# Reordering side tasks and partial products in a fused graph-attention kernel

## The chip, the cores and the metric

The kernel runs on one core of a Trainium2 chip. The metric is the device time of one execution in microseconds (us). Where two kernels are compared by a ratio, it is the mean time of one kernel's runs over the mean of the other's runs of the same rounds on the same chip, with a 95% interval. It is therefore not quite the quotient of the medians that stand beside it.

Engines: PE is TensorE (matrix products), DVE is VectorE, ACT is ScalarE, POOL is GpSimd, and SP is SyncE, whose queue (SPq) issues nearly all loads. An engine here starts its instructions in the order of its queue; what that costs is measured below (a write on VectorE that could have begun at 476.0 us began at 479.31, behind a norm that waited).

## The reference, cut to what matters

```python
# x: [128 graphs, 64 nodes, 512], float32; adj: [64, 64]
h = relu(layernorm(x))                           # input norm
def gat(h, W, a):                                # once with 4 heads, then once with 1
    Wh = h @ W
    e = leaky_relu(Wh @ a_left + (Wh @ a_right).T)
    return softmax(where(adj > 0, e, -1e9)) @ Wh
h   = elu(gat(h, W_heads, a_heads))              # 4 heads x 512 -> 2048 wide
out = elu(gat(h, W_out, a_out))                  # back to 512
y   = relu(out @ w1 + b1) @ w2 + b2 + out        # feed-forward
return x + layernorm(y) * gamma + beta           # gamma is 1 and beta 0 in these inputs
```

## The kernel before

The rows of x are cut into 64 tiles of 128 rows, four tiles to a group, 16 groups. A group passes through attention weights, a first projection (unit a, four heads), a second projection (unit b, 28 parts) and a feed-forward (units c and d). Products of 512 by 512 are made of seven smaller products instead of eight (numbered 1 to 7) with sums and differences of quarters around them; one small product is 8 matmuls. `unit` issues the seven in a given order and says what becomes of each:

```python
def after(p):                     # p: the product that has just been issued
    if p in (1, 5, 6):
        if p == 6:                # add product 1 to bank 6 (VectorE); then the copy "t"
            nc.vector.tensor_tensor(gb[6], gb[6], sb["s1"], ALU.add)
        nc.scalar.copy(sb[nm], gb[p])             # product 7 adds into bank 6 after this
        post(nm, sb[nm])
    elif p == 2: post("c11", gb[1])
    elif p == 7: post("c22", gb[6], sb["s5"], gb[1])   # an add on VectorE
    elif p == 3: post("c12", gb[5], sb["t"], gb[5])
    else:        post("c21", gb[6])                # product 4, in bank 6 behind c22's add
```

In unit a, product 4 of a head is issued only behind the second product of the next head. `run(steps, side)` spreads a list of side tasks evenly between the steps of a unit, and `mix` interleaves lists evenly. During the second projection of group g the side tasks are the feed-forward of group g-1 with its output norms, the attention sums of group g+1, and the input norms, scores, softmaxes and transposes of group g+2:

```python
# stage_a(g): side tasks of a later group; p and r are its two pairs of tiles
return [norms(p), norms(r), transposes(p), transposes(r), wait, project_f(g), wait, wait,
        (scores1(g), attn_weights(p)), None, attn_weights(r), wait, wait,
        transpose_weights(p), wait, wait, transpose_weights(r)]      # (shortened)
...
run(project2(g), mix(attn, tr) + mix(ff[:at] + early + ff[at:], stage_a(g + 2)) + fin)
```

`attn_weights` is a softmax on VectorE and ends with writing the weights `s1A`, which have one buffer. `transpose_weights` is a set of 8 transposes of `s1A` on TensorE (tile `s1pt`). `fin` are the four output norms, 7 instructions each:

```python
def finish(j):
    xr = load(t, "xr")                                     # the residual, on SyncE's queue
    nc.gpsimd.tensor_tensor(xr, xr, bs, ALU.add)           # the sum, GpSimd
    mean, rstd = norm_stats(y, "n2", t)                    # VectorE; the root (n2rs) on GpSimd
    nc.vector.scalar_tensor_tensor(y, y, mean, gs, ALU.subtract, ALU.mult)
    nc.vector.scalar_tensor_tensor(y, y, rstd, xr, ALU.mult, ALU.add)
    nc.sync.dma_start(out=of[ts(t, P), :], in_=y)
```

Of the kernel before, what the change touches and what calls it, by code (L numbers as in the profile page):

```python
# [22 lines left out]
def gat_preln_kernel(  # L23
# [38 lines left out]
    G = 4  # L62
# [178 lines left out]

    late = []

    def flush_late():
        while late:
            late.pop(0)()
# [148 lines left out]
    def scores1(g):  # L395

        L, R = LR.pop(g)
        pe = [aux([P, 2, H * N], f"s1pe{g}_{a}") for a in range(2)]
        for q in range(2):
            for a in range(2):  # L400
                for b in range(NB):
                    rows, cols = slice(64 * a, 64 * a + 64), slice(b * N, (b + 1) * N)
                    nc.tensor.matmul(
                        pe[a][cols, q, :].rearrange("p (h m) -> p h m", h=H), L[rows, q, cols],
                        R[rows, :, cols], start=(q == 0), stop=True, skip_group_check=True,
                    )
        for a in range(2):
            E1[2 * g + a] = pe[a].rearrange("p t (h m) -> p (t h) m", m=N)
# [67 lines left out]

    def stage_a(g):

        if g >= NG:
            return []  # L480
        p, r = 2 * g, 2 * g + 1

        def norms(p):
            norm1(2 * p)
            norm1(2 * p + 1)
            if p >= 2:
                prefetch(2 * p + 2)
                prefetch(2 * p + 3)

        def transposes(p):  # L490
            transpose_h(2 * p)
            transpose_h(2 * p + 1)

        wait = [lambda: None]
        return [
            lambda: norms(p), lambda: norms(r), lambda: transposes(p), lambda: transposes(r),
        ] + wait + [lambda: project_f(g)] + wait * 2 + [
            lambda: (scores1(g), attn_weights(p)), lambda: None, lambda: attn_weights(r),
        ] + wait * 2 + [lambda: transpose_weights(p)] + wait * 2 + [lambda: transpose_weights(r)]


    ZB = {}
# [54 lines left out]
    def project1(g, h):  # L557


        z = ZB[g]  # L560
        first = (g, h) == (0, 0)
        if h == 0:
            for b in ("11", "12", "S1", "22"):
                tag = "hS" if b == "S1" else "h" + b
                H1[b] = big.tile([P, H, 2, T], FP, tag=tag, name=f"h{b}_{g}")
        sums = {6: 0, 7: 1, 3: 2}
        blk = {1: "11", 2: "12", 4: "22", 5: "S1"}

        def post(what, a, b=None, to=None):
            if what[0] != "c":  # L570
                return
            nm = {"c11": "11", "c12": "12", "c21": "S1", "c22": "22"}[what]
            dst = H1[nm][:, h]
            if b is not None:
                nc.vector.tensor_tensor(to, a, b, ALU.add)  # L575
                a = to
            elu(flat(dst), flat(a), f"{what}_{g}_{h}")
            if what == "c21":
                nc.gpsimd.tensor_tensor(dst, dst, H1["22"][:, h], ALU.add)  # L579

        s = unit(
            f"a{g}_{h}", product_t(h, lambda p: ZSUM[h][sums[p]] if p in sums else z[blk[p]][:, h]),
            post, (1, 2, 6, 5, 7, 3, 4) if first else (1, 6, 5, 2, 7, 3, 4),
        )

        def next_sums():
            if h + 1 < H:
                z_sums(g, h + 1)

        return [  # L590
            s[0], lambda: (s[1](), flush_late()), lambda: (s[2](), next_sums()), s[3], s[4],
            lambda: (s[5](), late.append(s[6])),
        ]
# [90 lines left out]
    def feed_forward(g):  # L684

        o = OUT[g]
        OT, RT = [], []

        def transpose_out(j):
            if j % 2 == 0:  # L690
                OT.append(big.tile([P, KC, T], FP, tag=f"ot{j // 2}", name=f"ot{j // 2}_{g}"))
            pt = aux([P, KC, P], f"pto{g}_{j}")
            for k in range(KC):
                nc.tensor.transpose(pt[:, k, :], o[:, j, ts(k, P)], ident)  # L694
            nc.scalar.copy(OT[j // 2][:, :, ts(j % 2, P)], pt)
            nc.gpsimd.tensor_tensor(o[:, j], o[:, j], b2s, ALU.add)
            if j == G - 1:
                bl[1] = blocks(OT, f"o{g}")

        def blocks(tt, name):  # L700
            s2, s3, s4 = new_sums(name)
            a11, a12 = tt[0][:, 0:2], tt[0][:, 2:4]
            s1, a22 = tt[1][:, 0:2], tt[1][:, 2:4]
            nc.vector.tensor_tensor(s1, s1, a22, ALU.add)
            sums(nc.vector, s1, a11, a12, a22, s2, s3, s4)
            return {1: a11, 2: a12, 3: s4, 4: a22, 5: s1, 6: s2, 7: s3}

        bl = {}

        def post1(what, a, b=None, to=None):  # L710
            if what[0] != "c":
                return
            if not RT:
                RT.extend(big.tile([P, KC, T], FP, tag=f"rt{i}", name=f"rt{i}_{g}") for i in range(2))
            r, c = quadrant(what)
            dst = RT[r][:, 2 * c:2 * c + 2]
            if b is not None:
                nc.vector.tensor_tensor(dst, a, b, ALU.add)
                a = dst
            for k in range(2):  # L720
                nc.scalar.activation(
                    dst[:, k], a[:, k], AF.Relu, bias=b1s[:, 2 * c + k:2 * c + k + 1]
                )
            if what == "c21":
                bl[2] = blocks(RT, f"r{g}")

        def post2(what, a, b=None, to=None):

            if what == "s1":
                return  # L730
            r, c = {"t": (0, 1), "s5": (1, 1)}.get(what) or quadrant(what)
            dst = o[:, 2 * r:2 * r + 2, c * Q:(c + 1) * Q]
            eng = nc.vector if what[0] == "c" else nc.gpsimd
            eng.tensor_tensor(dst, a, dst, ALU.add)  # L734

        def finish(j):
            t = G * g + j
            xr = load(t, "xr")
            nc.gpsimd.tensor_tensor(xr, xr, bs, ALU.add)
            y = o[:, j]  # L740
            mean, rstd = norm_stats(y, "n2", t)
            nc.vector.scalar_tensor_tensor(y, y, mean, gs, ALU.subtract, ALU.mult)
            nc.vector.scalar_tensor_tensor(y, y, rstd, xr, ALU.mult, ALU.add)  # L743
            nc.sync.dma_start(out=of[ts(t, P), :], in_=y)

        f1 = unit(f"c{g}", product_t(M1, lambda p: bl[1][p]), post1, (1, 2, 6, 5, 7, 3, 4))
        f2 = unit(f"d{g}", product_n([M2], lambda p, i: bl[2][p]), post2, (1, 6, 5, 2, 3, 7, 4))
        return (
            [lambda j=j: transpose_out(j) for j in range(G)], f1 + f2,
            [lambda j=j: finish(j) for j in range(G)],  # L750
        )
# [59 lines left out]
    for g in range(NG):  # L811
        if g >= 1:
            side = stage_e(g - 1)
        else:
            side = stage_a(1)
            for i, m in ((6, 4), (11, 5), (16, 6), (21, 7)):
                side.insert(i, lambda m=m: more_sums(m))
        done, n = 0, 6 * H
        for i in range(n):
            if i % 6 == 0:  # L820
                steps = head0 if (g, i) == (0, 0) else project1(g, i // 6)
            if (g, i // 2) != (0, 0):
                steps[i % 6]()
            while done * n < (i + 1) * len(side):
                side[done]()
                done += 1
        flush_late()
        attn = attend1(g + 1) if g + 1 < NG else []
        if g >= 1:
            tr, ff, fin = feed_forward(g - 1)  # L830
        else:
            tr, ff, fin = [], [lambda: more_sums(M1), lambda: None, lambda: more_sums(M2), load_rows], []
        if g < NG - 1:
            early = [lambda: z_sums(g + 1, 0)]
            at = 8 if g >= 1 else 0
            run(project2(g), mix(attn, tr) + mix(ff[:at] + early + ff[at:], stage_a(g + 2)) + fin)
        else:
            run(project2(g), tr + [lambda: None] * 6 + ff[:2])
            run(ff[2:], [
                lambda: [scores2(g, j) for j in range(G)], lambda: spread2(g), lambda: None,  # L840
                lambda: None, lambda: softmax2(g),
                *[lambda: None] * 7, lambda: transpose_weights2(g), lambda: None,
                *[lambda j=j: attend2(g, j) for j in range(G)], lambda: None,
            ])
    last = fin
    tr, ff, fin = feed_forward(NG - 1)
    run(tr + ff[:6] + last + ff[6:12] + fin[:2] + ff[12:] + fin[2:])
# [29 lines left out]
```

## Time and profile before

| | before |
|---|---|
| median (3 runs) | 2395.09 us (2392.32 to 2395.43) |
| span of the profiled run | 2396.8 us |
| start: to the first product of group 1 | 195.5 us |
| middle: from there to the first product of group 15, 14 groups | 2016.1 us |
| end: the rest | 185.2 us |

The two marks are the first matmul of the first projection in the timeline of TensorE (at 195.53 and 2211.58 us). The windows view gives the busy time of each engine in a stretch (columns: stretch, its length, then busy us and instructions of PE, PEld, DVE, ACT and POOL, the granted clock, the DMA share, GB/s). For the middle of the kernel before:

```profile
195.50:2211.60 2016.10, 1995.47 (x10199) 1674.01 (x10198) 1100.05 (x1831) 776.97 (x1399) 842.50 (x725) 1.00 0.47 149
```

### The profile page before, as it was taken

How to read it: one execution, taken by the hardware profiler on the slowest of the kernel's cores; microseconds unless marked ns; L12 is line 12 of the kernel's file. 1: busy time of each engine (PE TensorE's matmuls, PEld its weight loads, DVE VectorE, ACT ScalarE, POOL GpSimd, SP SyncE). 2: the span in 40 equal slices, each digit the busy share in tenths (PEclk: the TensorE clock that was granted, in tenths of full speed). 3: DMA queues.
4: the chain of work that ended last, by engine and by line, in shares of the span. 5: the costliest groups of instructions: out<-in, count | busy, mean ns of one | idle time of the engine just before them, and what ended most of it. 6: DMA issues, size and time to landing. Idle time of an engine off the chain costs nothing.

```text
span 2396.8 us, 32990 instructions
## 1 busy us (share of the span) xinstructions
PE 2324.6 (97%) x11805; PEld 1941.5 (81%) x11805; DVE 1297.1 (54%) x2210; ACT 902.2 (38%) x1623; POOL 1030.2 (43%) x917
## 2 busy tenths in 40 slices
PE   6989999999999999999999999999999999999997
PEld 4768888888888788888888888888888888878785
DVE  6625375464745546364463745547465473734536
ACT  2524425253252533425244252533525244241512
POOL 5861544325344253443435443353443435433323
PEclk9999999999999999999999999999999999999999
DMA  8554454454545445454454544445454454534442
GB/s 300 193 177 142 129 175 131 146 165 131 172 128 154 151 136 171 132 171 132 139 169 134 174 132 154 153 134 176 130 173 133 136 171 132 176 118 156 152 148 94
DMA packets 257808, 366.89 MB, mean 153 GB/s; under 512 B 22216, under 2 KB 145128, under 8 KB 257648
## 3 DMA queue, kind: packets, MB, share of 16 engines
q1 hardware_dynamic: 251024, 343.82, 45.4%
q0 software_dynamic: 4512, 16.78, 1.9%
q10 hardware_dynamic: 2112, 4.19, 0.5%
q8 instruction: 95, 1.56, 0.3%
q14 instruction: 65, 0.53, 0.1%
HBM read 337.45 MB, written 27.26 MB: 152 GB/s over the span
## 4 chain that ended last, share of the span: by engine, by line
PE 84%; DVE 8%; DMA 3%; POOL 2%; issue 2%; ACT 1%; SPq 0%; DVEq 0%; POOLq 0%; ACTq 0%
PE g_b L319 30%; PE g_a L304 27%; PE g_c L304 8%; PE g_d L319 6%; PE pz L519 4%; PE pa L667 2%; DVE jf L633 2%; DVE o L743 2%; PE pzS L519 1%; PE pto L694 1%; PE pth L368 1%; DMA xr<-in_x_dram 1%; DMA x<-in_x_dram 1%; DVE n2st L340 1%; PE s1pt L469 1%
## 5 line engine op out<-in xcount | busy, mean ns | idle before, releaser
L319 PE MATMUL g_b<-w,h 128*128 128x256 f32 x2560 | 601.4, 381 | 0.0
L319 PEld LDWEIGHTS g_b<-w,h 128*128 128x128 f32 x2560 | 477.8, 190 | 74.6 <-issue 13.7
L304 PE MATMUL g_a<-zs_z,w 128*128 128x256 f32 x1504 | 353.9, 384 | 23.5 <-ACT t_a L270 23.1
L304 PE MATMUL g_a<-z,w 128*128 128x256 f32 x1520 | 360.2, 380 | 5.3 <-DVE g_a L575 4.3
L304 PEld LDWEIGHTS g_a<-zs_z,w 128*128 128x128 f32 x1504 | 287.5, 192 | 75.9 <-ACT t_a L270 29.3
L304 PEld LDWEIGHTS g_a<-z,w 128*128 128x128 f32 x1520 | 287.7, 190 | 60.7 <-issue 14.5
L319 PE MATMUL g_b<-w,hS 128*128 128x256 f32 x1024 | 246.4, 387 | 1.8 <-DVE z L531 1.8
L579 POOL TENSOR_TENSOR hS<-hS,h 128x512 f32<-128x512 f32 x64 | 82.9, 1296 | 340.4 <-DVE hS L543 340.4
L541 ACT ACTIVATE exc<-g_a 128x512 f32<-128x512 f32 x256 | 152.2, 595 | 201.4 <-DVE g_a L575 172.4
L319 PEld LDWEIGHTS g_b<-w,hS 128*128 128x128 f32 x1024 | 189.5, 191 | 45.4 <-issue 15.7
L543 DVE SCALAR_TENSOR_TENSOR h<-exc,g_a 128x512 f32<-128x512 f32 x192 | 131.8, 686 | 147.0 <-ACT exc L542 147.0
L609 POOL TENSOR_TENSOR h<-h,h 128x512 f32<-128x512 f32 x64 | 86.0, 1343 | 210.7 <-PE g_b L319 210.7
L542 ACT ACTIVATE exc<-exc 128x512 f32<-128x512 f32 x256 | 161.6, 631 | 6.6
L609 POOL TENSOR_TENSOR h<-hS,h 128x512 f32<-128x512 f32 x64 | 81.1, 1267 | 142.0 <-PE g_b L319 142.0
L329 POOL TENSOR_TENSOR zs_z<-zS,z 128x512 f32<-128x512 f32 x63 | 83.6, 1328 | 131.2 <-PE g_d L319 70.1
L330 POOL TENSOR_TENSOR zs_z<-z,zs_z 128x512 f32<-128x512 f32 x63 | 92.7, 1472 | 102.5 <-PE g_d L319 91.7
L633 DVE SCALAR_TENSOR_TENSOR jf<-wh,ao 128x512 f32<-128x512 f32 x128 | 120.0, 958 | 12.2 <-ACT wh L615 12.0
L331 POOL TENSOR_TENSOR zs_z<-z,zs_z 128x512 f32<-128x512 f32 x63 | 88.4, 1404 | 85.8 <-PE g_a L304 85.4
L319 PE MATMUL g_d<-w,rt 128*128 128x256 f32 x512 | 121.2, 379 | 1.8 <-DVE o L734 1.1
L304 PE MATMUL g_c<-ot,w 128*128 128x256 f32 x512 | 121.1, 379 | 0.7 <-ACT s_c L270 0.7
L304 PE MATMUL g_a<-zS,w 128*128 128x256 f32 x496 | 117.2, 379 | 0.0
L471 ACT COPY at<-s1pt 128x512 f32<-128x512 f32 x64 | 34.8, 589 | 211.4 <-PE s1pt L469 211.4
(159 smaller groups left out, 3550.8 us busy)
## 6 DMA issues: line engine op xcount, KB each, us to landing
w<-tc SPq DMA_DIRECT2D x632, 256.0 KB, 2.7
w<-in_L_gnn_W_heads_dram SPq DMA_DIRECT2D x192, 256.0 KB, 2.8
w<-in_L_gnn_W_out_dram SPq DMA_DIRECT2D x192, 256.0 KB, 2.7
w<-in_L_gnn_w_dram SPq DMA_DIRECT2D x96, 256.0 KB, 2.7
x<-in_x_dram SPq DMA_DIRECT2D x66, 256.0 KB, 2.8
xr<-in_x_dram SPq DMA_DIRECT2D x64, 256.0 KB, 3.0
out_dram<-o SPq DMA_DIRECT2D x64, 256.0 KB, 2.2
tc<-pt POOLq DMA_DIRECT2D x20, 512.0 KB, 5.0
```

The lines of the kernel that those rows point to most:

```text
L304: nc.tensor.matmul(bk[:, o, :], w[:, k, ts(o, P)], a[:, k, :], start=start and o == 0 and k == 0, stop=k == 1, skip_group_check=True,)
L319: nc.tensor.matmul(bk[:, j, :], a[:, k, ts(j, P)], w[:, k, :], start=start and k == 0 and j == 0, stop=i == len(ms) - 1 and k == 1, skip_g ...
L329: eng.tensor_tensor(s2, s1, a11, ALU.subtract)
L330: eng.tensor_tensor(s4, a12, s2, ALU.subtract)
L331: eng.tensor_tensor(s3, a22, s2, ALU.subtract)
L519: nc.tensor.matmul(banks[b][:, c, :].rearrange("p (h n) -> p h n", h=H), src[rows, off + c * P:off + (c + 1) * P], at[rows, b], start=True ...
L541: nc.scalar.activation(ex, src, AF.Relu, scale=-1.0)
L542: nc.scalar.activation(ex, ex, AF.Exp, scale=-1.0)
L543: nc.vector.scalar_tensor_tensor(dst, ex, -1.0, src, ALU.add, ALU.max)
L579: nc.gpsimd.tensor_tensor(dst, dst, H1["22"][:, h], ALU.add)
L609: nc.gpsimd.tensor_tensor(dst[:, h], x0[:, h], x1[:, h], ALU.subtract)
L633: nc.vector.scalar_tensor_tensor(junk, WH2[g][:, j], 1.0, ao[:, c, :], ALU.mult, ALU.mult, accum_out=f[:, c, j:j + 1],)
```

## The change

Its intent: the feed-forward and the output norms no longer stand at the end of the second projection's side tasks, so VectorE should reach the border to the next group's first projection with an empty queue. And the products come in a new order: in units a and c product 7 moves from fifth to sixth place, so it is due one product later. In unit c two products instead of one then lie between 6 and 7, for the add and the copy that 7 waits for; in unit a product 6 moves back as well, and two lie between them as before. In unit d product 7 was sixth already; there only 5 and 6 change places. Cut to its core:

```diff
-        wait = [lambda: None]
-        return [ ... one list ... ]                       # stage_a
+        return ([norms...], [transposes..., scores, attn_weights...],
+                [nothing, transpose_weights(p), nothing, nothing, transpose_weights(r)])
...
-            post, (1, 2, 6, 5, 7, 3, 4) if first else (1, 6, 5, 2, 7, 3, 4),   # unit a
+            post, (1, 2, 6, 5, 7, 3, 4) if first else (1, 5, 6, 2, 3, 7, 4),
-        f1 = unit(f"c{g}", ..., post1, (1, 2, 6, 5, 7, 3, 4))
-        f2 = unit(f"d{g}", ..., post2, (1, 6, 5, 2, 3, 7, 4))
+        f1 = unit(f"c{g}", ..., post1, (1, 5, 6, 2, 3, 7, 4))
+        f2 = unit(f"d{g}", ..., post2, (1, 5, 6, 2, 3, 7, 4))
...
-            run(project2(g), mix(attn, tr) + mix(ff[:at] + early + ff[at:], stage_a(g + 2)) + fin)
+        norms, scores, turns = stage_a(g + 2)
+        first = mix(attn, tr)
+        first[9:9] = norms[:1]
+        first += norms[1:]
+        if g == 0:                   # the sums of w1 and w2 come last, not in the middle
+            run(project2(g), first + early + scores + turns + [load_rows, sums(M1), sums(M2)])
+        else:
+            run(project2(g), first + mix(
+                ff[:7] + early + ff[7:12] + fin[:1] + ff[12:13] + fin[1:2] + ff[13:], scores
+            ) + mix(fin[2:], [nothing] + turns + [nothing] * 2))
```

More of the change, by code (lines that the diff above doesn't have):

```diff
@@ L242, in gat_preln_kernel, with nothing @@
     late = []
+    def nothing():
+        pass
     def flush_late():
@@ L479, in stage_a @@
         if g >= NG:
-            return []
+            return [], [], []
         p, r = 2 * g, 2 * g + 1
@@ L492, in transposes @@
             transpose_h(2 * p + 1)
-        wait = [lambda: None]
-        return [
-            lambda: norms(p), lambda: norms(r), lambda: transposes(p), lambda: transposes(r),
-        ] + wait + [lambda: project_f(g)] + wait * 2 + [
-            lambda: (scores1(g), attn_weights(p)), lambda: None, lambda: attn_weights(r),
-        ] + wait * 2 + [lambda: transpose_weights(p)] + wait * 2 + [lambda: transpose_weights(r)]
+        return (
+            [lambda: norms(p), lambda: norms(r)],
+            [
+                lambda: transposes(p), lambda: transposes(r), nothing, lambda: project_f(g), nothing,
+                lambda: (scores1(g), attn_weights(p)), nothing, lambda: attn_weights(r),
+            ],
+            [nothing, lambda: transpose_weights(p), nothing, nothing, lambda: transpose_weights(r)],
+        )
     ZB = {}
@@ L744, in finish @@
             nc.sync.dma_start(out=of[ts(t, P), :], in_=y)
-        f1 = unit(f"c{g}", product_t(M1, lambda p: bl[1][p]), post1, (1, 2, 6, 5, 7, 3, 4))
-        f2 = unit(f"d{g}", product_n([M2], lambda p, i: bl[2][p]), post2, (1, 6, 5, 2, 3, 7, 4))
+        f1 = unit(f"c{g}", product_t(M1, lambda p: bl[1][p]), post1, (1, 5, 6, 2, 3, 7, 4))
+        f2 = unit(f"d{g}", product_n([M2], lambda p, i: bl[2][p]), post2, (1, 5, 6, 2, 3, 7, 4))
         return (
@@ L814, in gat_preln_kernel @@
         else:
-            side = stage_a(1)
-            for i, m in ((6, 4), (11, 5), (16, 6), (21, 7)):
+            side = sum(stage_a(1), [])
+            for i, m in ((5, 4), (9, 5), (12, 6), (17, 7)):
                 side.insert(i, lambda m=m: more_sums(m))
@@ L828, in gat_preln_kernel, with sums_late @@
         attn = attend1(g + 1) if g + 1 < NG else []
-        if g >= 1:
-            tr, ff, fin = feed_forward(g - 1)
-        else:
-            tr, ff, fin = [], [lambda: more_sums(M1), lambda: None, lambda: more_sums(M2), load_rows], []
-        if g < NG - 1:
-            early = [lambda: z_sums(g + 1, 0)]
-            at = 8 if g >= 1 else 0
-            run(project2(g), mix(attn, tr) + mix(ff[:at] + early + ff[at:], stage_a(g + 2)) + fin)
-        else:
-            run(project2(g), tr + [lambda: None] * 6 + ff[:2])
-            run(ff[2:], [
-                lambda: [scores2(g, j) for j in range(G)], lambda: spread2(g), lambda: None,
-                lambda: None, lambda: softmax2(g),
-                *[lambda: None] * 7, lambda: transpose_weights2(g), lambda: None,
-                *[lambda j=j: attend2(g, j) for j in range(G)], lambda: None,
-            ])
+        norms, scores, turns = stage_a(g + 2)
+        tr, ff, fin = feed_forward(g - 1) if g >= 1 else ([], [], [])
+        if g == NG - 1:
+            run(project2(g), tr + [nothing] * 6 + ff[:2])
+            run(ff[2:], [
+                lambda: [scores2(g, j) for j in range(G)], lambda: spread2(g), nothing, nothing,
+                lambda: softmax2(g), *[nothing] * 7, lambda: transpose_weights2(g), nothing,
+                *[lambda j=j: attend2(g, j) for j in range(G)], nothing,
+            ])
+            continue
+        early = [lambda: z_sums(g + 1, 0)]
+        first = mix(attn, tr)
+        first[9:9] = norms[:1]
+        first += norms[1:]
+        if g == 0:
+            def sums_late(m):
+                fetch(m)
+                weight_sums(m, LAST["A"])
+            run(project2(g), first + early + scores + turns + [
+                load_rows, lambda: sums_late(M1), lambda: sums_late(M2)
+            ])
+        else:
+            run(project2(g), first + mix(
+                ff[:7] + early + ff[7:12] + fin[:1] + ff[12:13] + fin[1:2] + ff[13:], scores
+            ) + mix(fin[2:], [nothing] + turns + [nothing] * 2))
     last = fin
```

## The prediction

> **What bounds the kernel now.** I read the busy table first, then TensorE's waits, then the timeline around the longest repeated wait.
>
> ```profile
> PE 2324.6 (97%) x11805; PEld 1941.5 (81%) x11805; DVE 1297.1 (54%) x2210; ACT 902.2 (38%) x1623; POOL 1030.2 (43%) x917
> ```
>
> TensorE sets the end; the instructions on it do not change, so only its gaps can be won: 2396.8 - 2324.6 = 72 us in all. The waits say who owns them (columns: total us, times, longest):
>
> ```profile
> PE g_a L304 <- ACT t_a L270: 23.1, 14, 3.2
> ...
> PE g_a L304 <- DVE g_a L575: 4.3, 3, 3.0
> PE pz L519 <- DVE z L531: 3.8, 1, 3.8
> PE g_c L304 <- ACT t_c L270: 3.0, 1, 3.0
> ...
> PE g_b L319 <- DVE z L531: 1.8, 1, 1.8
> ```
>
> The first row has 14 cases, one for each border between a second projection and the next group's first projection, except the first border (group 0 has no feed-forward behind it). The repeating block is 144.35 us long (from 338.16 to 482.51 and so on); one border in TensorE's timeline:
>
> ```profile
> 482.15 1.89 PE L304 MATMUL g_a<-z,w 128*128 128x256 f32 x8
> 483.88 1.89 PE L304 MATMUL g_a<-zs_z,w 128*128 128x256 f32 x8
> 485.61 1.89 PE L304 MATMUL g_a<-zS,w 128*128 128x256 f32 x8
> 487.33 1.89 PE L304 MATMUL g_a<-z,w 128*128 128x256 f32 x8
> 490.92 3.72 PE L304 MATMUL g_a<-zs_z,w 128*128 128x256 f32 x16 [1.70 <-ACT t_a L270]
> ```
>
> The reader sees products 1, 6, 5, 2 of the first head, 1.73 us apart, and product 7 late by 1.86 us (487.33 + 1.73 = 489.06). It waits for the copy of the sum of bank 6, and that sum stands last in this VectorE queue:
>
> ```profile
> 485.51 0.75 DVE L743 SCALAR_TENSOR_TENSOR o<-o,n2rs,xr 128x512 f32<-128x512 f32 x1 [0.44 <-POOL n2rs L346]
> 486.18 1.76 DVE L633 SCALAR_TENSOR_TENSOR jf<-wh,ao 128x512 f32<-128x512 f32 x1
> ...
> 488.48 0.68 DVE L340 BATCH_NORM_STATS2 n1st<-x 128x6 f32<-128x512 f32 x1
> ...
> 489.50 0.70 DVE L269 TENSOR_TENSOR g_a<-g_a,s_a 128x512 f32<-128x512 f32 x1
> ```
>
> So output norms of the last feed-forward (L743), scores (jf) and input statistics hold up the add at the border. The last border is worse:
>
> ```profile
> 2221.80 6.56 PE L304 MATMUL g_a<-zs_z,w 128*128 128x256 f32 x16 [3.15 <-ACT t_a L270]
> ```
>
> After 3.15 us idle the same 16 matmuls take 6.56 instead of 3.72 us, and the windows view grants a clock of 0.55 there; after 1.70 us it grants 1.00.
>
> [...] the trace agrees in kind (clock 0.55 after 3.15 us, none lost after 2.0). [...]
>
> ```profile
> 474.07 1.68 DVE L743 SCALAR_TENSOR_TENSOR o<-o,n2rs,xr 128x512 f32<-128x512 f32 x1
> ...
> 477.00 0.74 DVE L743 SCALAR_TENSOR_TENSOR o<-o,n2rs,xr 128x512 f32<-128x512 f32 x1
> ```
>
> The first ran beside a GpSimd sum (473.94 to 475.20), the second did not.
>
> **The change, part by part.** (a) The order 1, 5, 6, 2, 3, 7, 4 moves product 7 of a head from fifth to sixth. Product 6 also moves one later, so two products still lie between them, but everything at the border gets 1.73 us more. Product 7 was due 4 x 1.73 = 6.9 us after the head's first matmul, so its add had to start by 5.5 (1.37 is add, copy and hand-overs: 489.50 to 490.87), and it started after 7.35 (489.50 - 482.15); now it may start after 7.26. This alone nearly removes the wait. (b) The feed-forward products now end before product 4 of the second projection begins, and in the built VectorE order the four output norms stand ahead of the copy of the second s1A, no longer behind the border. What is left there is three dot products, two input statistics, two more dot products and then the add: 7 x 0.65, plus one wait for the last input load (2.8 us to landing, issued after the last norm is stored) and one for the last quarter of the projection; by that count VectorE is ready some 3 us before product 6 has ended. By both, the border wait should vanish: 23.1 us plus 0.16 us of drain at each of 14 borders, 2.3, plus 2.84 for the slow clock after the last: 28.2 us.
>
> (c) What it adds: the second softmax of each group and its transposes (s1pt) now stand beside the norms, and the transposes stand only one product before the projection's last two parts. Before, they had much room:
>
> ```profile
> 461.77 0.20 DVE L429 RECIPROCAL s1r<-s1s 128x8 f32<-128x8 f32 x1
> ...
> 465.94 0.69 DVE L432 TENSOR_TENSOR s1A<-s1e,s1r 128x512 f32<-128x512 f32 x1 [0.18 <-PE s1pt L469]
> 477.82 1.04 PE L469 MATMUL s1pt<-ident,s1A 128*128 128x128 f32 x8
> ```
>
> The last line is from the timeline of TensorE: the weights were ready 11 us early. In the new order TensorE has 11 products and one set of transposes between the scores (s1pe) and this second set: 11 x 1.73 + 0.87 = 19.9 us. In the same stretch VectorE has, in the built order and ahead of the write of s1A (line numbers are those of before): the first softmax up to its reciprocal (4.3 us, as from 451.05 to 455.33 before), 15 full-size operations at 0.60 (start to start where nothing waits), four statistics at 0.60, four L742-type at 0.66, small ones 1.2 and s1A itself 0.69: 4.3 + 9.0 + 2.4 + 2.6 + 1.2 + 0.7 = 20.2 us. The last of each four transposes also needs the copy after it, behind another norm: 21.1, when TensorE, after three transposes, would be at 20.2. So without any contention it loses 0.9 us. I add an estimate of 1.5: one L743 blocked by GpSimd's z sum (0.5), one L742 by the addition to xr (0.75), the rest in smaller waits for n2rs (about 0.95 us each on GpSimd). That makes 2.4 us in each of groups 1 to 13: 13 x 2.4 = 31 us. It is one in-order queue against another: the built order puts the transposes there, and TensorE cannot pass them.
>
> (d) Group 0: the sums of w1 and w2 leave the busy start. The waits of 1.8 (g_b) and 3.8 us (pz) near 137 and 143 us are GpSimd and DMA held by the fetch of w2 (6.83 us wait for it), and the next eight matmuls took 3.53 instead of 1.89. Of 7.2 us I take 6.5; the sums land in a stretch where GpSimd idles (172 to 199 us).
> (e) The last feed-forward: product 7 waited 3.04 us for t_c with one product between 6 and 7; now two. With the slow clock after it (1.7) and a new 0.7 to 2 us before product 6, I take 3.5 us off.
>
> Sum: -28.2 + 31 - 6.5 - 3.5 = -7 us: 2388.
>
> **The rivals.** First, clean gain: VectorE keeps up, the transposes lose nothing or the 0.9 us that the count gives. For it: 20.2 against 19.9 us is a near tie, and somebody tuned this order. Then 13 x 0.9 - 38 = -26: 2369. Second, the new wait takes over and goes past 3 us, where the clock falls as at the last border. For it: [...] the xr loads (3.0 us to landing) come in series with norms. Then 3.3 + 2.8 = 6.1 each, 79 - 38 = +41: 2436. Third, nothing shifts but the order: product 4 now follows 7 by two products instead of three, so c22's add has 3.45 instead of 5.2 us; where it waited already (4.3 us in three places) it may wait up to 1.73 more, about +5 us in all. The border wait staying is the least likely: the delay beyond its slack was 1.86 us and (a) alone gives 1.73.
>
> **Range and chances.** The only large term is the s1pt wait, 13 times something between 0.5 and 3.5 us, so each microsecond is worth 13. I put the middle at 2386, slightly below the sum since an order that was kept probably measured well, and 8 of 10 chances in 2362 to 2420. Faster by over 2% (below 2347) would need more than the whole 38 us of removable waits: 0.02. Slower by over 2% (above 2443) needs the clock to fall in nearly every group: 0.05. Within 2%: 0.93.
>
> **What would show it.** Right: TensorE's waits lose the row g_a after t_a (below 3 us in total), and a new row s1pt after s1A of VectorE appears 13 times, 1 to 3 us each; pz and g_b after z vanish; the group period goes from 144.35 to about 145. Wrong: no s1pt row (then the VectorE count is too high and the first rival holds); g_a after t_a still tens of us; windows with a clock near 0.55 in every group (second rival); g_a after its add L575, now a later line, with over 10 us (third).

## The result, and the profile after

| | before | after |
|---|---|---|
| median (6 runs each, same rounds) | 2395.17 us (2392.32 to 2395.9) | 2410.22 us (2403.6 to 2418.48) |
| ratio | | 1.0065, 95% interval 1.0043 to 1.0087 |
| span of the profiled run | 2396.8 us | 2401.8 us |
| start / middle / end | 195.5 / 2016.1 / 185.2 us | 193.4 / 2034.1 / 174.3 us |

The change costs 0.65%. The middle has become 18 us longer, the end 11 us shorter. The profiled run is the quickest of the six, so it shows the smallest loss; a second profile follows below. The busy line and TensorE's waits of the changed kernel (columns: us in total, times, longest):

```profile
PE 2328.6 (97%) x11805; PEld 1942.7 (81%) x11805; DVE 1205.2 (50%) x2210; ACT 911.5 (38%) x1623; POOL 1026.3 (43%) x917
```

```profile
PE s1pt L472 <- DVE s1A L435: 31.5, 14, 5.4
PE pzS L525 <- DVE z L537: 6.2, 1, 6.2
...
PE s1pt L472 <- DVE s1A L439: 3.0, 10, 1.3
...
PE g_a L307 <- DVE g_a L581: 0.7, 1, 0.7
```

The row g_a after t_a, 23.1 us before, is gone. In its place stands s1pt after s1A: 31.5 us, of which one case of 5.4 us is the start-up's, as before; 26.1 us remain in 13 groups, and the 3.0 us after L439 belong to the same transposes. VectorE's busy time fell from 1297.1 to 1205.2 us on the way, and TensorE gained nothing by it. The middle in the windows view:

```profile
193.40:2227.50 2034.10, 2004.97 (x10198) 1678.75 (x10197) 1015.68 (x1834) 785.43 (x1398) 848.30 (x735) 1.00 0.46 149
```

TensorE idles 29.1 us there, 8.5 more than before, and is busy 9.5 us longer with one matmul less on record. So half of the middle's loss is idle time and the other half is work that ran slower. One border in TensorE's timeline shows both:

```profile
480.14 0.52 PE L472 MATMUL s1pt<-ident,s1A 128*128 128x128 f32 x3 [2.38 <-DVE s1A L435]
480.85 1.33 PE L472 MATMUL s1pt<-ident,s1A 128*128 128x128 f32 x5 [0.19 <-DVE s1A L439]
481.97 4.64 PE L322 MATMUL g_b<-w,h 128*128 128x256 f32 x16
...
493.36 3.62 PE L307 MATMUL g_a<-zs_z,w 128*128 128x256 f32 x16
```

The last line holds products 3 and 7 behind the border, where the wait of the kernel before stood: none is left. Ahead of the second set of transposes TensorE waits 2.38 us, and the 16 matmuls of the projection's last parts then take 4.64 us, at a granted clock of 0.78 (windows view, 481.97 to 486.61), where the same number takes 3.62 us at 1.00 (493.36 to 496.98). Why s1A is late stands in VectorE's timeline, and behind it in GpSimd's:

```profile
473.93 0.16 DVE L432 RECIPROCAL s1r<-s1s 128x8 f32<-128x8 f32 x1
474.01 0.11 DVE L347 TENSOR_SCALAR n2ve<-n2mv 128x1 f32<-128x1 f32 x1
...
477.31 0.75 DVE L749 SCALAR_TENSOR_TENSOR o<-o,n2rs,xr 128x512 f32<-128x512 f32 x1 [1.93 <-POOL n2rs L349]
...
479.31 0.69 DVE L435 TENSOR_TENSOR s1A<-s1e,s1r 128x512 f32<-128x512 f32 x1
```

```profile
475.50 1.27 POOL L745 TENSOR_TENSOR xr<-xr,bs 128x512 f32<-128x512 f32 x1 [2.07 <-DVE wh L623]
476.72 0.55 POOL L349 TENSOR_TENSOR n2rs<-n2ve,mhalf 128x1 f32<-128x1 f32 x1
```

The reciprocal that the write of s1A (L435) needs is ready at 474.1 us, and its one buffer is free when the first set of transposes has read it, at 476.0 us (TensorE, 475.00 + 1.04). But the write stands behind the third output norm (L749), which waits 1.93 us for its root (n2rs). The root's own input (n2ve) is also ready at 474.1; but in GpSimd's queue the root stands behind the sum of the fourth tile's residual, which begins only at 475.50. So a root of 0.55 us began at 476.72, 2.6 us after its input was ready, and VectorE and TensorE waited in turn.

### The profile page after: what moved, and what is told of

It is laid out like the page before. It is cut to its first block, busy times and chain, and to the rows that moved or that the text cites. A ratio compares the mean times of both kernels' runs of the same rounds, so it can differ in the third digit from the quotient of the medians.

```text
span 2401.8 us, 32882 instructions
## 1 busy us (share of the span) xinstructions
PE 2328.6 (97%) x11805; PEld 1942.7 (81%) x11805; DVE 1205.2 (50%) x2210; ACT 911.5 (38%) x1623; POOL 1026.3 (43%) x917
## 4 chain that ended last, share of the span: by engine, by line
PE 82%; DVE 10%; DMA 2%; issue 2%; POOL 2%; ACT 1%; SPq 0%; DVEq 0%; POOLq 0%
PE g_a L307 31%; PE g_b L322 25%; PE g_c L307 8%; PE g_d L322 5%; PE pz L525 4%; PE pa L673 2%; DMA xr<-in_x_dram 2%; DVE o L749 2%; DVE o L748 2%; PE pzS L525 1%; PE pto L700 1%; PE pth L371 1%; DVE n2st L343 1%; DVE s1A L435 1%; DVE o L740 1%
## 5 line engine op out<-in xcount | busy, mean ns | idle before, releaser
L307 PE MATMUL g_a<-zs_z,w 128*128 128x256 f32 x1504 | 347.8, 379 | 0.0
L333 POOL TENSOR_TENSOR zs_z<-z,zs_z 128x512 f32<-128x512 f32 x63 | 87.6, 1391 | 116.9 <-PE g_d L322 74.2
L745 POOL TENSOR_TENSOR xr<-xr,bs 128x512 f32<-128x512 f32 x64 | 84.3, 1318 | 76.8 <-DMA xr<-in_x_dram 70.3
L322 PEld LDWEIGHTS g_d<-w,rt 128*128 128x128 f32 x512 | 96.0, 190 | 17.3 <-DVE o L740 1.4
L428 ACT ACTIVATE s1e<-s1e 128x512 f32<-128x512 f32 x32 | 20.2, 630 | 232.1 <-DVE s1e L427 232.1
```

Source lines behind the costliest of these rows:

```text
L307: nc.tensor.matmul(bk[:, o, :], w[:, k, ts(o, P)], a[:, k, :], start=start and o == 0 and k == 0, stop=k == 1, skip_group_check=True,)
L322: nc.tensor.matmul(bk[:, j, :], a[:, k, ts(j, P)], w[:, k, :], start=start and k == 0 and j == 0, stop=i == len(ms) - 1 and k == 1, skip_g ...
L333: eng.tensor_tensor(s4, a12, s2, ALU.subtract)
```

## The experiments

Every run below is right unless it says otherwise. The table gives all of them, with start, middle and end as defined above, and the idle time of TensorE in the middle (length less busy time from the windows view).

| kernel | median us | ratio to before | 95% interval | start / middle / end us | idle in the middle |
|---|---|---|---|---|---|
| before (first profile) | 2395.17 | 1 | | 195.5 / 2016.1 / 185.2 | 20.6 |
| changed (first profile) | 2410.22 | 1.0065 | 1.0043 to 1.0087 | 193.4 / 2034.1 / 174.3 | 29.1 |
| changed, again | 2414.85 | 1.0057 | 1.0040 to 1.0074 | 193.7 / 2042.2 / 174.5 | 30.3 |
| product orders alone | 2382.90 | 0.9928 | 0.9913 to 0.9942 | 197.3 / 2011.8 / 174.3 | 15.2 |
| side tasks alone | 2406.33 | 1.0026 | 1.0008 to 1.0043 | 187.5 / 2038.3 / 178.7 | 27.1 |
| constant rows (wrong result) | 2361.60 | 0.9842 | 0.9826 to 0.9858 | 192.6 / 1992.2 / 174.5 | 0.0 |
| root ahead of the sum | 2393.65 | 0.9974 | 0.9959 to 0.9989 | 192.1 / 2026.3 / 176.9 | 23.0 |
| no sum | 2371.70 | 0.9891 | 0.9878 to 0.9904 | 192.2 / 2004.5 / 172.9 | 7.2 |
| before with the late sums of group 0 | 2390.73 | 0.9960 | 0.9945 to 0.9975 | 184.9 / 2019.0 / 181.6 | 21.9 |
| changed, four loads elsewhere | 2402.21 | 1.0019 | 1.0005 to 1.0034 | 185.0 / 2039.0 / 174.3 | 29.4 |
| transposes later | 2377.70 | 0.9904 | 0.9889 to 0.9919 | 189.9 / 2007.2 / 174.5 | 9.9 |
| transposes later, root ahead | 2370.73 | 0.9878 | 0.9859 to 0.9897 | 192.5 / 1998.3 / 176.9 | 3.0 |
| all three edits | 2364.75 | 0.9862 | 0.9848 to 0.9876 | 186.5 / 1998.9 / 176.9 | 3.6 |

My theory after the result: the border wait went away by both parts of the change, and the second softmax, now standing behind the output norms in VectorE's queue, costs more than was won. The rival: the new wait only stands in front of other waits for a VectorE queue that is late anyway, and taking it away would win little.

### The two halves of the change

Product orders alone (the kernel before with the three new orders):

```diff
-            post, (1, 2, 6, 5, 7, 3, 4) if first else (1, 6, 5, 2, 7, 3, 4),
+            post, (1, 2, 6, 5, 7, 3, 4) if first else (1, 5, 6, 2, 3, 7, 4),
# and units c and d as in the change
```

> Only the product orders of the changed kernel, with the side tasks of the kernel before. My theory (order and side tasks each remove the border wait; only the new place of the second softmax costs time): the row g_a after t_a falls from 23.1 us (14 cases) to under 4 us, no row of s1pt after s1A of 1 us or more apart from the start-up's 5.4 us, the period of a group falls from 144.35 to about 142.5 us, and the time is 2365 to 2372 us. Rival A (the order alone is not enough, the border wait needs the side tasks): the row keeps more than 10 us and the time is 2380 us or more. Rival B (product 4 after 7 by two products instead of three costs as much): a row g_a after its own add of over 10 us, time about 2395 us.

Measured: 2382.90 us, ratio 0.9928. TensorE's waits of this run:

```profile
PE g_a L304 <- DVE g_a L575: 15.2, 12, 2.1
...
PE g_a L304 <- ACT t_a L270: 0.6, 1, 0.6
```

The order alone does take away the wait for the copy t_a. But in 12 groups the next user of the late VectorE queue now waits, product 4, which needs the add of c22 (L575); that is rival B, and it takes 15.2 of the 23.1 us back. VectorE's timeline at a border of this run:

```profile
494.22 0.69 DVE L340 BATCH_NORM_STATS2 n1st<-x 128x6 f32<-128x512 f32 x1 [2.68 <-DMA x<-in_x_dram]
...
495.24 1.36 DVE L633 SCALAR_TENSOR_TENSOR jf<-wh,ao 128x512 f32<-128x512 f32 x1
...
498.68 0.69 DVE L575 TENSOR_TENSOR g_a<-g_a,s_a 128x512 f32<-128x512 f32 x1
```

It stands 2.68 us at the input statistics of a tile whose load is issued only after the last output norm, and reaches the add at 498.68, when TensorE had wanted the result at 498.0. My expectation of 2365 to 2372 us missed: I had the first wait right and did not follow the queue on to the next one. By the table, most of what this kernel wins is at the end (10.9 us, against 4.3 in the middle).

Side tasks alone (the changed kernel with the three old orders):

```diff
-            post, (1, 2, 6, 5, 7, 3, 4) if first else (1, 5, 6, 2, 3, 7, 4),
+            post, (1, 2, 6, 5, 7, 3, 4) if first else (1, 6, 5, 2, 7, 3, 4),
# and units c and d as in the kernel before
```

> Only the side tasks of the changed kernel, with the product orders of before. My theory (the side tasks alone both remove the border wait and add the s1pt wait): no row g_a after t_a above 3 us (VectorE had 3.3 us to spare at the border, and the old order takes 1.73 of that), s1pt after s1A 26 us in 13 cases as in the changed kernel, time 2402 to 2415 us. Rival (the border wait went through the order): g_a after t_a returns with 10 to 23 us on top of the s1pt wait, time 2420 to 2435 us.

Measured: 2406.33 us, as expected. No wait at any border in the middle, and s1pt after s1A is 24.6 us in 13 groups plus 2.5 after L439. So the side tasks both remove the border wait and bring the new one. With them in place the new orders win nothing at the borders; what they win is at the end (178.7 against 174.3 us), where product 7 of unit c no longer waits 3.0 us.

### Taking the new wait away

The second set of transposes of groups 1 to 13 reads constant rows instead of s1A. The result is wrong; the instructions stay the same.

```diff
-                nc.tensor.transpose(to, A[:, j, h:h + 2].rearrange("p b m -> p (b m)"), ident)
+                rows = A[:, j, h:h + 2].rearrange("p b m -> p (b m)")
+                if p % 2 == 1 and p >= 7:
+                    rows = gs[:, h * N:(h + 2) * N]
+                nc.tensor.transpose(to, rows, ident)
```

> The changed kernel, but the second set of transposes of each group (groups 1 to 13) reads constant rows instead of s1A: wrong result on purpose, same instructions, the wait for s1A is gone. My theory (this wait is the whole of what the change adds): the rows s1pt after s1A fall from 29.1 to at most 3 us beside the start-up's, the clock stays at 1.0 behind the transposes, and the time falls by 29 us of idle time and 5 to 12 us of lowered clock: 2366 to 2378 us. Rival (it only stands in front of another wait for the same late VectorE queue: scores, the border or the next s1pe waits instead): the time falls by less than 15 us, 2395 us or more.

Measured: 2361.60 us, ratio 0.9842. In the middle TensorE has no idle time left, and the groups take 142.70 us each (for instance 478.10 to 620.80; only the last of the middle is shorter, 136.96). The rival falls: nothing else was hidden behind this wait. The gain is larger than I expected: 42.5 us between the two profiled runs, and some 48 us on the medians (of different chips). The part above the idle time needed a second profile of the changed kernel.

### The changed kernel once more

No edit; a second profile, on another chip.

> The changed kernel once more, without an edit, for a second profile and a ratio on the same chip as the two after it: ratio to the kernel before 1.004 to 1.009, s1pt after s1A about 26 us in 13 groups beside the start-up's 5.4 us. The start-up's wait (pzS after z, 6.2 us in the first profile) is expected to change by some microseconds from run to run if it is a matter of when loads land, and to stay within half a microsecond if it belongs to the program.

Measured: ratio 1.0057, s1pt after s1A 26.6 us in 13 groups. The start-up's wait is 6.5 us (6.2 in the first profile, and 5.0 to 5.7 in the five later runs with the same start), so it belongs to the program, though its size varies. But the middle took 2042.2 us, 8 more than in the first profile, with nearly the same idle time. Two rows of the windows view, each 8 us long and beginning at the end of a wait, behind waits of 2.16 and 1.74 us:

```profile
481.60:489.60 8.00, 7.81 (x32) 6.66 (x33) 5.20 (x17) 1.76 (x3) 0.00 (x0) 0.79 0.47 158
...
922.20:930.20 8.00, 7.80 (x39) 6.78 (x40) 5.54 (x17) 2.25 (x4) 0.00 (x0) 1.00 0.61 186
```

The column after POOL's instructions is the granted clock: 0.79 in the first, 1.00 in the second, with 32 matmuls done against 39. This happened in 9 of the 13 groups of this profile and in 5 of 13 of the first. What it costs: the two groups with these borders took 147.14 and 145.05 us; the waits differ by 0.42, so 1.67 us are the clock. The clock records in the traces, from which the view takes its mean, hold only 1.00 and 0.50 here, and each fall behind these waits lasts 3.41 us at 0.50 (480.63 to 484.04 us in the first profile). The 0.79 over 8 us is the same: (1 - 0.79) x 8 / 0.5 = 3.4 us at 0.50. By that estimate a fall costs half of 3.4, 1.7 us, and 1.67 are measured. In the first profile 5 x 1.7 = 8.5 of the 9.5 us of longer busy time are this; in the second 9 x 1.7 = 15 of 2011.92 - 1995.47 = 16.5.

How long a wait must be is not sharp by its length alone. In the two profiles no wait of 1.74 us or less lowered the clock (with the side tasks alone one of 1.54 us did). Of those between 1.78 and 2.56 us some did and some did not (2.56 and 2.10 did not, 1.78 did). The clock records show more than the lengths do. In the profiles of the kernels before and after, all changes of the clock lie, within 4 ns, on one grid of 3.413 us, whose place differs between the two. Cut into the cells of this grid, the time from 200 to 2300 us shows 2 and 5 falls from 1.00, each at the end of a cell in which TensorE had idled 1.90 to 2.49 us in sum. The other cells at 1.00 had at most 1.96 us and were followed by 1.00. Over all 13 profiles I counted 40 falls; the least idle time in a cell ahead of one was 1.73 us, and the most in a cell without one 1.96 us. The windows view shows single cells of the first profile of the changed kernel: behind 1.90 us of idle time (623.99 to 627.40, 1.52 busy) the clock was 0.50, behind 1.95 us (330.44 to 333.86, 1.47 busy) it stayed at 1.00. The second is where most of the wait of 2.56 us lies (331.90 to 334.46): a border of the grid, at 333.86, divides it.

### What the lateness of s1A is made of

First, swap one pair of instructions in GpSimd's queue in the changed kernel: the third norm's root ahead of the fourth tile's sum.

```diff
-            nc.gpsimd.tensor_tensor(xr, xr, bs, ALU.add)
+            add = nc.gpsimd.tensor_tensor(xr, xr, bs, ALU.add)
+            if j == 3:          # queue it behind the root of tile 2
+                tc.add_manual_dep(add.ins, LAST["rstd"].ins.name, NoSync, reason="...")   # (shortened)
```

> The changed kernel, but on GpSimd the root for the third output norm of each group goes ahead of the sum for the fourth tile's residual (one pair of instructions swapped in GpSimd's queue; the orders of all other engines stay). My theory (s1A is late because VectorE's in-order queue stands 1.9 us at the third norm, whose root waits behind a sum that waits for its load): the wait of 1.93 us of the norm goes, s1A comes 1.5 to 1.9 us earlier, s1pt after s1A falls from 26 to 2 to 7 us in 13 groups, the clock stays at 1.00 behind it, and the ratio to the kernel before falls to 0.985 to 0.993. Rival A (VectorE has simply too many instructions there[...]): s1pt keeps 15 us or more and the ratio stays above 0.998. Rival B (the fourth norm waits instead, as its sum comes later): the same as A for s1pt.

Measured: ratio 0.9974, and s1pt after s1A 19.6 us in 13 groups. Both my theory and its rivals were too simple. The wait of 1.93 us at the third norm is gone, but the sum now runs while VectorE works, as GpSimd's and VectorE's timelines of the same border show:

```profile
475.06 1.66 POOL L745 TENSOR_TENSOR xr<-xr,bs 128x512 f32<-128x512 f32 x1 [0.32 <-DMA xr<-in_x_dram]
```

```profile
475.57 1.69 DVE L755 SCALAR_TENSOR_TENSOR o<-o,n2mv,gs 128x512 f32<-128x512 f32 x1
```

The fourth norm's instruction takes 1.69 instead of 0.74 us, so 0.95 us of the gain is given back: beside a sum on GpSimd (475.06 to 476.72) it is as slow as the norm in the prediction (1.68 us beside a sum, 0.74 without). In ten groups the wait fell from about 2.0 to 1.3 us. It is worth more than that: none of these ten lost clock (their periods are all 144.6 us), and the middle became 15.9 us shorter than in the second profile of the changed kernel, of the same chip and rounds, of which only 7.3 us are idle time. Against the first profile, in which the clock fell less often, it is 7.8 us, of which 6.1 are idle time.

Second, leave the sum out (beta is zero in these inputs, so the result is right, but it is no general kernel):

```diff
-            nc.gpsimd.tensor_tensor(xr, xr, bs, ALU.add)
+            pass
```

> The changed kernel without the sum of beta and the residual on GpSimd (beta is zero in these inputs, so the result stays right; it is no general kernel). It takes away both things that the run with the root ahead of the sum left over: the root waiting behind a sum, and the sum's blocking of VectorE's norms (1.69 instead of 0.74 us in the fourth). Theory (these two are the whole of the lateness of s1A): s1A comes 2.5 to 3 us earlier than in the changed kernel, s1pt after s1A falls below 6 us beside the start-up's, no lowered clock, group period about 143, ratio to the kernel before 0.985 to 0.990. Rival (VectorE has too many instructions for the place, as my count of 0.9 us said): 0.9 us stay in each of 13 groups, 12 us in all, ratio 0.990 to 0.995.

Measured: ratio 0.9891, and 7.2 us of wait in 13 groups (4.7 for the write of s1A and 2.5 for the copy after it). The same border in TensorE's timeline:

```profile
474.74 0.52 PE L472 MATMUL s1pt<-ident,s1A 128*128 128x128 f32 x3 [0.37 <-DVE s1A L435]
475.45 0.77 PE L472 MATMUL s1pt<-ident,s1A 128*128 128x128 f32 x5 [0.19 <-DVE s1A L439]
```

So of some 2.2 us per group, about 1.6 come from the sum, through the queue or through slower instructions of VectorE beside it (1.69 instead of 0.74 us above). The remaining 0.56 is VectorE's own work: from 457.9 us until it writes s1A at 473.91 its timeline shows no wait. One norm in it takes 1.10 instead of 0.74 us beside another GpSimd sum (463.22 to 465.07), so a part of the 0.56 may be this slowing again; it was not separated. The result lies between the theory (below 6 us) and the rival (12 us): VectorE does have slightly too much to do there, as the prediction counted (0.9 us), but the sum is the larger part.

### The start-up

The prediction took 6.5 us off the start; measured were 2.1 us (195.5 to 193.4) and a new wait of 6.2 us. The kernel before with only the late sums of w1 and w2 in group 0 (the sums of W_out in unit a of group 0, which the change also moves, stay where they were):

```diff
-            tr, ff, fin = [], [lambda: more_sums(M1), lambda: None, lambda: more_sums(M2), load_rows], []
+            run(project2(g), attn + [lambda: z_sums(g + 1, 0)] + stage_a(g + 2) + [
+                load_rows, lambda: sums_late(M1), lambda: sums_late(M2)
+            ])
+            continue
```

> The kernel before with only the change's part for group 0: the sums of w1 and w2 and the row loads go to the end of the second projection of group 0. My prediction's step (d): the waits of pz and g_b after z near 137 and 143 us vanish and 6.5 us are won, ratio 0.9973 or less. The rival that the changed kernel's profile suggests (the wait is for loads of x, issued late by SyncE behind loads of weight sums): a wait of 5 to 7 us after z stays in the start-up, ratio 0.999 to 1.002.

Measured: ratio 0.9960, and group 1 begins at 184.9 instead of 195.5 us. The rival that I took from the profile falls: this part of the change by itself wins what was predicted and more. The table's column of starts says what ate it: 187.5 us with the side tasks alone, 197.3 with the orders alone, 193.4 with both. The new orders lengthen the start. How sure that is: six further runs have the changed kernel's start as it is (its second profile, and five whose edits come later), and with the first profile their starts spread from 189.9 to 193.7 us, so the 187.5 us without the new orders lie below all seven, but the 1.8 us between 195.5 and 197.3, and the 2.1 us that the change wins, are no more than this spread. Where the time stands in the changed kernel, by SyncE's queue and by VectorE:

```profile
106.44 24.81 SPq L238 DMA_DIRECT2D w<-tc  x8
131.35 0.38 SPq L238 DMA_DIRECT2D w<-in_L_gnn_W_out_dram  x1
131.84 0.41 SPq L95 DMA_DIRECT2D x<-in_x_dram  x1
```

```profile
137.81 0.69 DVE L343 BATCH_NORM_STATS2 n1st<-x 128x6 f32<-128x512 f32 x1 [12.56 <-DMA x<-in_x_dram]
```

Eight loads of weight sums hold SyncE's queue for 24.8 us (18.5 us of it waiting for one store of such sums, 12.8 us in the kernel before); the load of x behind them leaves at 131.84 us, and VectorE stands 12.56 us at its statistics, with copies behind it that TensorE needs. The test is to issue these loads of x from another engine's queue, in the changed kernel:

```diff
-        nc.sync.dma_start(out=tl, in_=xf[ts(t, P), :])
+        queue = nc.scalar if name == "x" and 12 <= t < 16 else nc.sync
+        queue.dma_start(out=tl, in_=xf[ts(t, P), :])
```

> The changed kernel, but the loads of four tiles of x (12 to 15) in the start-up are issued from ScalarE's queue and no longer stand behind SyncE's loads of weight sums. Theory (the start-up's new wait, pzS after z, is VectorE standing 12 us at the statistics of x, whose load stands in SyncE's queue behind loads that wait for a store): the wait of 6.2 us falls below 1.5 us, the eight matmuls after it take 1.99 instead of 3.78 us, group 1 begins at 184 to 188 instead of 193 us, ratio 1.002 to 1.004 where the changed kernel has 1.006. Rival (the copies of z wait for something else, such as the memory traffic of the weight sums): the wait stays over 4 us, ratio unchanged.

Measured: ratio 1.0019, group 1 at 185.0 us. The wait fell from 6.2 to 2.29 us, not below 1.5; the eight matmuls of the projection that follow took 2.88 us (2.75 in the changed kernel, where eight from 144.89 us take 1.99 at a granted clock of 1.00), so that part of the expectation missed. But 8.4 us of start-up are won, by no longer queueing four loads behind others. That the new orders let SyncE reach the loads of sums at a less lucky time is read from the traces (26.4 us with the orders alone, 21.6 with the side tasks alone) and was not tested by itself.

### Towards a better kernel

Transposes two products later:

```diff
-            ) + mix(fin[2:], [nothing] + turns + [nothing] * 2))
+            ) + mix(fin[2:], [nothing] * 3 + turns))
```

> The changed kernel with both sets of transposes two products later in the second projection (the second set after the third instead of the first of the last products). My theory (the weights come 2 to 2.5 us too late for the place where the transposes stand, and two products are 3.5 us): s1pt after s1A falls below 5 us beside the start-up's, no new wait above 5 us, time 2366 to 2378 us, below both kernels. Rival (the lateness moves along, since s1A's buffer and the next tasks depend on the transposes, or the border add now waits behind the copies): another row grows by 10 us or more, time 2390 us or more.

Measured: 2377.70 us, ratio 0.9904, waits for s1pt in the middle 8.0 us, of which 6.7 are for s1A where I had expected less than 5. The time is in the expected range, though some lateness moves along. The same with the root ahead of the sum:

> Both: the root ahead of the sum, and the transposes two products later. It is the candidate to beat both kernels. If the two edits act on the same lateness, the remaining 7 us of waits in the kernel with late transposes vanish (s1pt after s1A below 1 us in 13 groups) and the time comes to that of the kernel with constant rows, ratio 0.983 to 0.987. If something else limits it, the ratio stays at the 0.990 of the late transposes alone.

Measured: 2370.73 us, ratio 0.9878. The waits for s1pt are gone in all groups but one (1.75 us); the ratio stayed just above the expected 0.983 to 0.987. The end has grown by 2.4 us (176.9 against 174.5), as in all three kernels with the root ahead; why was not looked into. With the four loads of x from ScalarE's queue added:

> All three edits together (transposes two products later, root ahead of the sum, four loads of x from ScalarE's queue): candidate for the best right kernel. If the gains add, ratio 0.9878 less 0.003, 0.984 to 0.986, median 2360 to 2366 us. If the start-up's gain is given back later, it stays at 0.9878.

Measured: 2364.75 us, ratio 0.9862, 1.4% below the kernel before and 2.0% below the changed one (0.9862 / 1.0065), in the expected range of time (the ratio is a trace above the expected 0.986). One border of it:

```profile
468.81 3.62 PE L323 MATMUL g_b<-w,h 128*128 128x256 f32 x16
472.26 1.34 PE L473 MATMUL s1pt<-ident,s1A 128*128 128x128 f32 x8
473.43 1.89 PE L308 MATMUL g_a<-z,w 128*128 128x256 f32 x8
```

No wait is left here, neither at the transposes nor at the border; the one of 1.75 us in the last group stays. A second buffer for s1A, another way out, was not tried.

## Why the prediction was right or wrong

The time fell into the range and into "within 2%", but the sum had the wrong sign: a gain of 7 us (9 after the last shading) where 15 were lost. A range of 58 us held both signs, so that the time fell into it says little for the sum; the mechanisms can be checked one by one. By its steps, beside the first profile:

| part | predicted | measured |
|---|---|---|
| middle: border wait in 13 of the 14 borders | -22 (19.95 of wait, 2.1 of drain) | -20.0 of wait, gone in all |
| middle: s1pt after s1A | +31 | +29.1 of wait |
| middle: clock behind it | 0 | +9.5 busy time (16.5 in the second profile) |
| start, step (d) | -6.5 | -2.1 |
| end: last border (3.15 + 0.16 + 2.84) and step (e) (3.5) | -9.6 | -10.9 |

Step (a), "This alone nearly removes the wait", holds for the wait that it names (0.6 us left with the orders alone). It would have been worth far less than that by itself, since the third rival then takes 15.2 us; I had given it 5. In the changed kernel the side tasks keep it at 0.7 us.

Step (b), that the border wait vanishes, was right, in size too.

Step (c) was right in kind, place and size: 13 groups, 2.4 us each predicted, about 2.2 measured. The parts of the sum were less good. I gave 0.9 us to the count of instructions, 1.25 to two slowed beside GpSimd and 0.25 to small waits for the roots; one wait of 1.93 us for one root, queued behind a sum on another engine, makes up most of it. Without the sum 0.56 us are left where I had counted 0.9.

The term that was missing from the sum is the clock. I wrote of the kernel before: "clock 0.55 after 3.15 us, none lost after 2.0", and so put the fall of the clock into a rival beyond 3 us. The same profile shows otherwise. Two windows behind border waits of 1.97 and 2.06 us in the kernel before:

```profile
635.60:643.60 8.00, 7.98 (x29) 6.71 (x30) 5.88 (x12) 3.28 (x6) 2.75 (x2) 0.79 0.51 173
782.10:790.10 8.00, 7.93 (x36) 6.68 (x37) 5.77 (x11) 2.31 (x5) 3.29 (x3) 1.00 0.72 247
```

I had looked at a case like the second and taken it for the rule. So the second rival came true in part, with waits of about 2 us and in 5 and 9 of the 13 groups, beside the sum and not in place of it. With 13 waits of about 2.2 us it cost some 8.5 us in one profile and 15 in the other, by the estimate above; this fits the changed kernel's runs spreading over 15 us where those of the kernel before spread over 4 in the same rounds.

Step (d), "Of 7.2 us I take 6.5", failed in the sum though not in its cause: moving the sums of w1 and w2 wins 10.6 us of start by itself. What I did not price was that the rest of the change, by the runs above the product orders, lengthens the start again. The place of the wait is shown (loads of x in SyncE's queue behind loads that wait for a store; issued elsewhere, they win 8.4 us); that the orders put it there is read from the traces only. Of my signs, the waits of g_b and pz went, but one of 6.2 us for the same copies of z came at pzS.

Putting the middle 2 us below my own sum "since an order that was kept probably measured well" had no measurement behind it and went the wrong way.

## What to carry to other kernels

A task moved out of one wait in an in-order queue lands ahead of something else in it: follow the queue on to the next thing that the bounding engine needs, on every engine that the task touches (here a root on GpSimd behind a sum, begun 2.6 us after its input was ready, and a load on SyncE behind eight others that held the queue for 24.8 us). When TensorE is the bound, price a repeated wait by its length and by the clock behind it: cutting ten of thirteen waits from 2.0 to 1.3 us was worth more than twice the idle time saved, on the same chip (15.9 against 7.3 us), and none of the ten then lost clock. The best order here leaves each consumer a margin of one or two products, rather than putting it where the producer just about arrives.
